# Last inverses on another queue, tables ahead of an exchange, softmax sums behind a score tile

## The chip, the cores and the metric

The kernel runs on one core of a Trainium2 chip. Five engines work side by side, each through a list of instructions in a fixed order, and wait for each other through semaphores: TensorE (PE in the profile; its weight loads are PEld), VectorE (DVE), ScalarE (ACT), GpSimd (POOL) and SyncE (SP). SyncE does nothing here but issue DMAs; GpSimd issues DMAs and does a few elementwise operations. The metric is device time in microseconds from start to end of one execution, as the median of several runs.

## The reference

Two layers stand one behind the other, in float32. The input x has 4 batches of 1024 channels by 1024 pixels (32 x 32); `_rmsnorm` takes the root mean square over all 1024 features.

```python
x = hidden_states.reshape(B, C, N).transpose(0, 2, 1)
qkv = (x @ w_qkv.T + b_qkv).reshape(B, N, 3, nh, hd)        # 16 heads of 64
q, k = _apply_rope(q, cos, sin), _apply_rope(k, cos, sin)   # pairs of features turned by tables
q = _rmsnorm(q.reshape(B, N, inner), q_norm_w).reshape(B, N, nh, hd)
k = _rmsnorm(k.reshape(B, N, inner), k_norm_w).reshape(B, N, nh, hd)
scores = jnp.einsum('bqhd,bkhd->bhqk', q, k) * scale
attn = jax.nn.softmax(scores, axis=-1)
ctx = jnp.einsum('bhqk,bkhd->bqhd', attn, v).reshape(B, N, inner)
out = _rmsnorm(ctx @ w_proj.T, norm_out_w) + residual
```

The second layer is a bottleneck block on the result: a 1x1 convolution to 256 channels, a 3x3 convolution, a 1x1 convolution back to 1024, each followed by a normalisation over the batch, and a scaled residual. The change does not touch it.

## The kernel before

**Stages.** For each batch the kernel makes q, k and v (three projections), then the attention, then the output projection (y). In the profile the products of these are p_q, p_k, p_v, sc and cx (attention) and p_y. Features lie on partitions, 128 to a block, and eight blocks f make the 1024 features; a block holds two heads and is called a head pair, hp. The projections save products by Strassen-like sums: `project2` runs seven outer products k, each of seven inner ones of four matmuls, with sums of weights (made once and kept in DRAM, `wd` and `wd2`) and sums of right-hand sides that VectorE makes just ahead (L450 to L454 for the inner, L281 to L284 for the outer sums). The seven weight tiles of one outer product come from a ring of eight buffers (`wring`), so the next product's weights are loaded as the tiles of the last one are used up. SyncE issues these loads.

**Attention.** It is in two halves c of 512 query pixels and eight head pairs each, sixteen steps for a batch. In a step TensorE makes eight score tiles (L787), each for 128 keys and both heads; ScalarE takes the exponential (L794); VectorE adds the eight results into a tile of partial sums d_ (L798, L800); then TensorE makes the product with v from the same exponentials (cx, L808). What is missing is the sum over the 128 partitions, also a TensorE product, with a tile of ones: `dn`. Four heads (two steps) share one such product (L841), right behind the second step's cx. In the first half of each batch it is done for eight heads at once instead (L861): `halve` first folds each tile's upper partitions onto its lower ones by DMAs on GpSimd's queue (L852 to L855), into tiles called `fold`.

**Inverses.** ScalarE copies dn to SBUF (L891); the rows travel through DRAM (`dens`) into a small tile, VectorE inverts that (`few`), and it travels back; `spread` then loads each inverse onto the 32-partition groups of a tile (inv, eight DMAs), VectorE multiplies the attention's result with it (L764) and GpSimd adds v's bias (L765). All these DMAs are on SyncE. For the last four heads of a batch the detour is left out: VectorE inverts the whole tile (L893), SyncE stores it and spreads it straight from SBUF (L894, L910). This happens within the output projection of that batch, which needs the result for its later products.

**Rotary tables.** `rope` multiplies q (or k) with the sine table into a second tile and with the cosine table in place (`turn`, L718 to L725), then adds the first to the second with partitions swapped, by an accumulating DMA on GpSimd (L727, the exchange). The tables are first multiplied with the inverse root mean square (L715), which destroys them, so behind the last block of each turn GpSimd loads them again (`load_tables`, L176 and L177). `pace["tables"]` keeps the next rope's first step from being put into VectorE's list too early after that load.

**Weight parts.** During batch 0's attention 21 sets of weight sums for later are made (`prepare_blocks`, `prepare`): SyncE loads four tiles, VectorE makes four sums, and the last argument names the queue that stores them.

**Order.** TensorE's, VectorE's, ScalarE's and GpSimd's lists are in the order in which the program writes them. The program hangs VectorE's work of the projections onto product counts (`after`, `waiting`, `pace`). SyncE's list is ordered when the program is built. TensorE's result banks are three score tiles of two banks each, one bank for cx and one for dn.

Of the kernel before, what the change touches and what calls it, by code (L numbers as in the profile page):

```python
# [11 lines left out]
F32 = mybir.dt.float32  # L12
# [6 lines left out]
P = 128  # L19
B, C, H, W = 4, 1024, 32, 32  # L20
N = H * W
NT = C // P
HD = 64
NHP = C // (2 * HD)
CH = 512
# [36 lines left out]
NH = NT // 2  # L62
NG = NT // 2
QH = P // 4
# [21 lines left out]
def program(ctx, tc, x, wblk, w2, w3, vecs, cos, sin, out, bad):  # L86


    nc = tc.nc
# [26 lines left out]
    def col(name, i=0):  # L116
        return vec[:, COL[name] + i : COL[name] + i + 1]
# [40 lines left out]
    with tc.tile_pool(name=f"st{u}", bufs=2) as st, ExitStack() as s:  # L158
# [11 lines left out]
        cosT = tp.tile([P, N], F32, tag="cos", name="cosT")  # L170
        sinT = tp.tile([P, N], F32, tag="sin", name="sinT")

        def load_tables(queue):
            for i in range(2):

                queue.dma_start(sinT[i::2, :], sin[1 - i :: 2, :])  # L176
            queue.dma_start(cosT, cos)  # L177

        ident = None
# [23 lines left out]
        def bank(kind, name):  # L203
            pool, shape = psum[kind]
            return pool.tile(shape, F32, tag=kind, name=name)
# [503 lines left out]
        def rope(b, dst, total, eps, scale, w, tag, biased=True):  # L709

            def tables():
                for t in (sinT, cosT):
                    nc.vector.tensor_tensor(t, t, total, ALU.mult)  # L715

            def turn(f):
                k, other = dst[:, f, :], big_temp(f"{tag}s_{b}_{f}")  # L718
                for i, (t, table) in enumerate(((other, sinT), (k, cosT))):
                    if w is not None:  # L720
                        nc.vector.scalar_tensor_tensor(t, k, w[i][:, f : f + 1], table, ALU.mult, ALU.mult)
                    elif biased:
                        nc.vector.tensor_tensor(t, k, table, ALU.mult)
                    else:
                        nc.vector.scalar_tensor_tensor(t, k, col("bq", f), table, ALU.add, ALU.mult)  # L725
                for i in range(2):
                    nc.gpsimd.dma_start(dst[i::2, f, :], other[1 - i :: 2, :], accum_op=ALU.add)  # L727
                if f == NT - 1 and (b, tag) != (B - 1, "k"):
                    load_tables(nc.gpsimd)
                    pace["tables"] = pace["at"] + 3.7  # L730

            def then():
                if pace["at"] < pace["tables"]:
                    after(pace["tables"] - pace["at"], then)
                    return
                waiting.append((4 * TT, tables))
                for f in range(NT):
                    waiting.append((4 * TT, lambda f=f: turn(f)))

            inverse_rms(total, eps, scale, f"{tag}_{b}", then)  # L740
# [26 lines left out]
        def attention(b, c, q_all, k_all, v, probs_, late, ready, extra, slow, steps_in_all, load_parts, fold):  # L767


            at = half[c]  # L770
            sums_ = []
            for hp in range(NHP):
                n = f"{b}_{c}_{hp}"
                if late:
                    late.pop(0)()
                rows = shifts(q_all, k_all, n, hp, c) if bad is None else None
                probs = []
                if fold and hp % 2 == 0:
                    d_ = fold[hp // 4][:, hp % 4 // 2 * 2 : hp % 4 // 2 * 2 + 2, :]
                else:  # L780
                    d_ = acc.tile([P, 2, CH], F32, tag="tot", name=f"den_{n}")
                for t in range(N // P):
                    p = probs_[:, t]
                    sc = bank("sc", f"sc_{n}_{t}")
                    for j in range(2):
                        d = slice(j * HD, (j + 1) * HD)
                        nc.tensor.matmul(  # L787
                            sc[:, j], k_all[d, hp, t * P : (t + 1) * P], q_all[d, hp, at],
                            start=True, stop=bad is not None,
                        )  # L790
                    if bad is None:
                        for j in range(2):
                            nc.tensor.matmul(sc[:, j], ones[0:1, :], rows[j], start=False, stop=True)
                    nc.scalar.activation(p, sc, AF.Exp)  # L794
                    if t == 3:
                        load_parts()
                    if t == 1:
                        nc.vector.tensor_tensor(d_, probs[0], p, ALU.add)  # L798
                    elif t > 1:
                        nc.vector.tensor_tensor(d_, d_, p, ALU.add)  # L800
                    probs.append(p)
                if eights and eights[0][0] <= c * NHP + hp:
                    eights.pop(0)[1]()
                o = bank("cx", f"cx_{n}")
                for t in range(N // P):
                    for j in range(2):
                        h0 = (2 * hp + j) * HD
                        nc.tensor.matmul(  # L808
                            o[j * HD : (j + 1) * HD, :], v[:, t, h0 : h0 + HD], probs[t][:, j],
                            start=(t == 0), stop=(t == N // P - 1),  # L810
                        )

                nc.scalar.copy(q_all[:, hp, at], o)  # L813
                sums_.append(d_)
                if hp % 2 == 1:
                    for r in ready:
                        mean_of_v(q_all, *r)
                    ready.clear()
                if fold:
                    halve(hp, d_, fold[hp // 4][:, hp % 4 // 2 * 2 : hp % 4 // 2 * 2 + 2, :])  # L820
                    if hp % 4 == 3:
                        eights.append((hp + 2, lambda n=n, hp=hp: sum_of_eight(b, n, hp, fold[hp // 4], ready)))
                if half_done and half_done[0][0] <= c * NHP + hp:
                    half_done.pop(0)[1]()
                if slow:
                    slow.pop(0)()

                if waiting:
                    next_waiting()
                slots = NCH * NHP - 1  # L830
                if extra and steps_in_all == 0 and hp > 0:
                    extra.pop(0)()
                for _ in range(len(extra) - -(-steps_in_all * max(slots - 1 - c * NHP - hp, 0) // slots) if steps_in_all else 0):
                    extra.pop(0)()
                if hp % 2 == 0 or fold:
                    continue
                dn = bank("dn", f"dn_{n}")
                for i, d_ in enumerate(sums_):
                    for j in range(2):
                        q = slice((2 * i + j) * QH, (2 * i + j + 1) * QH)  # L840
                        nc.tensor.matmul(dn[q, :], ones[:, :QH], d_[:, j], start=True, stop=True)  # L841
                sums_ = []
                late.append(lambda *a, n=n, hp=hp, dn=dn: inverses(b, c, hp, n, dn, ready))

        half_done, eights = [], []
        low, high = slice(0, P // 2), slice(P // 2, P)
# [38 lines left out]
        def inverses(b, c, hp, n, dn, ready):  # L885


            r = temp(f"rec_{n}")
            k = 2 * ((b * NCH + c) * NHP + hp - 1)

            nc.scalar.copy(r, dn)  # L891
            if (c, hp) == (NCH - 1, NHP - 1):
                nc.vector.reciprocal(r, r)  # L893
                nc.sync.dma_start(dens[k : k + 4, :], r[::QH, :])  # L894
                spread(c, hp, n, ready, [r[q * QH : (q + 1) * QH, :] for q in range(4)])
                return
            few, rows = to_few(n, k, 4, r[::QH, :])

            def invert():
                nc.vector.reciprocal(few, few)  # L900
                nc.sync.dma_start(rows, few)
                spread(c, hp, n, ready, [dens[k + q, :].partition_broadcast(QH) for q in range(4)])

            half_done.append((0, invert))

        def spread(c, hp, n, ready, rows):
            w = big_temp(f"inv_{n}")
            for i in range(2):
                for j in range(4):
                    nc.sync.dma_start(w[j * QH : (j + 1) * QH, half[i]], rows[2 * i + j // 2])  # L910
                ready.append((c, hp - 1 + i, w[:, half[i]]))

        def o_norm(b, total, ys):
# [245 lines left out]
        load_x(0, 0, range(NH, NT))  # L1159
        w1 += [block(WQ, g, 1, f"q_0_{g}_1") for g in range(NG)]  # L1160
        load_x(0, 1)
        load_tables(nc.sync)
        queue_sums(ts[0], xs[0])
        room = v_room("rq_0")
        for b in range(B):
# [45 lines left out]
            def load_parts():  # L1211

                while todo and len(made) < 2:
                    made.append(todo.pop(0)(pieces, nc.sync, nc.sync))

            extra = [lambda: made.pop(0)()] * len(todo)
            load_parts()
# [8 lines left out]
            slow = [lambda: None] * 3 + [lambda f=f: add_residual(f) for f in range(NT)] if b > 0 else []  # L1226
            probs_ = xp.tile([P, N // P, 2, CH], F32, tag="x", name=f"p_{b}")

            fold = [[tp.tile([P, NH, CH], F32, tag=t, name=f"den_{b}_{t}") for t in ("T0", "T2")], None]
            for c in range(NCH):  # L1230
                if (b, c) == (B - 1, NCH - 1):
                    extra = filters()
# [433 lines left out]
```

## Time and profile before

| | |
|---|---|
| median of 3 runs | 2677.93 us (2675.83 to 2679.2) |
| the profiled execution's own time | 2679.37 us |
| its span, first to last instruction | 2677.6 us |
| TensorE busy | 2646.0 us, 99% |
| VectorE busy | 2112.0 us, 79% |
| ScalarE busy | 1113.8 us, 42% |
| GpSimd busy | 434.3 us, 16% |

The batches' attention stages lie at 288 to 522, 865 to 1096, 1442 to 1673 and 2018 to 2249 us; the output projection follows each. In a row of the profile "p_y L485 <- DMA w_y<-wdf" says that the instruction of line 485 that writes p_y waited for a DMA that fills w_y from wdf. A matmul in float32 shows as two records. Names ending in f (wdf, wd2f, densf) are DRAM tensors of the program.

### The profile page before, as it was taken

What the parts mean: (1) busy time and instruction counts of PE and PEld (TensorE: products, weight loads), DVE (VectorE), ACT (ScalarE), POOL (GpSimd) and SP (SyncE); (2) the same over time, 40 slices, a digit from 0 to 9 for tenths busy, and PEclk for the clock granted to TensorE, in tenths of its full rate; (3) what the DMA queues carried; (4) which work ended last, traced back from release to release, by engine and by line L of the source; (5) the groups of instructions that cost most, each with busy time, mean ns of one, the idle gap of its engine ahead of it and who ended that gap; (6) DMA issues with size and microseconds to landing.
All of it is one profiled execution on the core that took longest, in us unless ns stands there. A gap on an engine that the chain in (4) does not pass through costs nothing. (4 is left out here: it accounts for less than half of the span.)

```text
span 2677.6 us, 32431 instructions
## 1 busy us (share of the span) xinstructions
PE 2646.0 (99%) x11322; PEld 1652.9 (62%) x11322; DVE 2112.0 (79%) x2536; ACT 1113.8 (42%) x1551; POOL 434.3 (16%) x501
## 2 busy tenths in 40 slices
PE   9999999999999999999999999999999999999997
PEld 4448533488888333688886333888884335846843
DVE  5668989997888766888878767887978679877987
ACT  2222455423442555333343555233525554312266
POOL 2542202100111222100111222100111222010000
PEclk9999999999999999999999999999999999999999
DMA  7887787767667551556775441665774443593165
GB/s 279 289 253 216 223 239 239 239 201 221 201 186 204 96 92 34 166 156 218 194 199 131 92 79 30 213 204 175 192 212 87 80 103 105 163 279 115 64 232 208
DMA packets 261387, 462.37 MB, mean 173 GB/s; under 512 B 34528, under 2 KB 127248, under 8 KB 261216
## 3 DMA queue, kind: packets, MB, share of 16 engines
q1 hardware_dynamic: 222048, 328.75, 39.3%
q0 software_dynamic: 39168, 131.45, 20.7%
q8 instruction: 93, 1.52, 0.2%
q14 instruction: 78, 0.64, 0.1%
HBM read 327.43 MB, written 97.01 MB: 159 GB/s over the span
## 5 line engine op out<-in xcount | busy, mean ns | idle before, releaser
L794 ACT ACTIVATE p<-sc 128x1024 f32<-128x1024 f32 x512 | 476.7, 1047 | 26.5 <-PE sc L787 25.8
L787 PE MATMUL sc<-q,k 64*128 64x512 f32 x2048 | 457.7, 596 | 0.0
L800 DVE TENSOR_TENSOR den<-den,p 128x1024 f32<-128x1024 f32 x288 | 356.1, 1236 | 30.4 <-DVE den L800 0.5
L787 PEld LDWEIGHTS sc<-q,k 64*128 64x128 f32 x2048 | 189.9, 186 | 265.2 <-issue 121.7
L808 PE MATMUL cx<-p,to 128*64 128x512 f32 x1536 | 340.2, 595 | 0.0
L808 PEld LDWEIGHTS cx<-p,to 128*64 128x64 f32 x1536 | 106.0, 137 | 228.8 <-issue 228.8
L480 PE MATMUL p_v<-w_v,x 128*128 128x256 f32 x928 | 211.7, 382 | 2.8 <-DVE x L451 2.8
L485 PE MATMUL p_y<-q,w_y 128*128 128x256 f32 x928 | 209.8, 379 | 0.0
L765 POOL TENSOR_SCALAR q<-q,vec 128x512 f32<-128x512 f32 x64 | 128.2, 2014 | 436.3 <-DVE q L764 436.3
L480 PEld LDWEIGHTS p_v<-w_v,x 128*128 128x128 f32 x928 | 177.3, 191 | 28.6 <-DVE x L451 3.9
L485 PEld LDWEIGHTS p_y<-q,w_y 128*128 128x128 f32 x928 | 176.0, 190 | 27.1 <-issue 3.4
L813 ACT COPY q<-cx 128x512 f32<-128x512 f32 x64 | 37.6, 587 | 360.7 <-PE cx L808 360.7
L798 DVE TENSOR_TENSOR den<-p 128x1024 f32<-128x1024 f32 x48 | 59.7, 1245 | 117.5 <-ACT p L794 117.5
L485 PE MATMUL p_q<-to,w_q 128*128 128x256 f32 x672 | 152.2, 379 | 0.0
L485 PE MATMUL p_k<-to,w_k 128*128 128x256 f32 x672 | 152.2, 379 | 0.0
L485 PEld LDWEIGHTS p_q<-to,w_q 128*128 128x128 f32 x672 | 127.4, 190 | 18.4 <-issue 1.2
L485 PEld LDWEIGHTS p_k<-to,w_k 128*128 128x128 f32 x672 | 127.4, 190 | 18.4 <-issue 1.2
L800 DVE TENSOR_TENSOR den_T<-den_T,p 128x1024 f32<-128x1024 f32 x96 | 117.6, 1226 | 10.4 <-ACT p L794 0.5
L808 PE MATMUL cx<-p,rq 128*64 128x512 f32 x512 | 113.4, 595 | 0.0
L1570 PE MATMUL c<-h,w 128*128 128x512 f32 x256 | 110.3, 592 | 0.5 <-ACT h L1473 0.5
L485 PE MATMUL p_y<-to,w_y 128*128 128x256 f32 x384 | 91.3, 383 | 5.8 <-DMA w_y<-wdf 5.8
L480 PE MATMUL p_v<-w_v,t 128*128 128x256 f32 x384 | 90.2, 379 | 0.9 <-DMA w_v<-wdf 0.8
(488 smaller groups left out, 4205.0 us busy)
## 6 DMA issues: line engine op xcount, KB each, us to landing
w_v<-wd2f SPq DMA_DIRECT2D x112, 256.0 KB, 3.3
w_y<-wd2f SPq DMA_DIRECT2D x112, 256.0 KB, 2.8
w_q<-wd2f SPq DMA_DIRECT2D x84, 256.0 KB, 2.7
w_k<-wd2f SPq DMA_DIRECT2D x84, 256.0 KB, 2.7
wd2f<-w_pre SPq DMA_DIRECT2D x68, 256.0 KB, 2.7
x<-in_x_dram SPq DMA_DIRECT2D x64, 256.0 KB, 5.0
q<-qs POOLq DMA_DIRECT2D x64, 256.0 KB, 5.5
k<-ks POOLq DMA_DIRECT2D x64, 256.0 KB, 4.4
```

Source lines behind the costliest of these rows:

```text
L480: nc.tensor.matmul(o[:, q].rearrange("p (g f) -> p g f", g=2), r[:, i, q * P : (q + 1) * P], wt[:, :, i, :], skip_group_check=True, **at,)
L485: nc.tensor.matmul(o[:, q], wt[:, q, i, :], r[:, i, :], skip_group_check=True, **at)
L765: nc.gpsimd.tensor_scalar(cx, cx, col("bv", hp), None, ALU.add)
L787: nc.tensor.matmul(sc[:, j], k_all[d, hp, t * P : (t + 1) * P], q_all[d, hp, at], start=True, stop=bad is not None,)
L794: nc.scalar.activation(p, sc, AF.Exp)
L798: nc.vector.tensor_tensor(d_, probs[0], p, ALU.add)
L800: nc.vector.tensor_tensor(d_, d_, p, ALU.add)
L808: nc.tensor.matmul(o[j * HD : (j + 1) * HD, :], v[:, t, h0 : h0 + HD], probs[t][:, j], start=(t == 0), stop=(t == N // P - 1),)
L813: nc.scalar.copy(q_all[:, hp, at], o)
L1570: nc.tensor.matmul(os[i], w3t[k][f // NH][:, f % NH, :], h2[b, k][:, half[c]], start=(k == 0), stop=(k == NPT - 1),)
```

## The change

- The last inverses of a batch: the store to `dens` and the eight loads of `spread` are issued by GpSimd instead of SyncE.
- Tables: `load_tables` is split. The sines are loaded directly behind VectorE's last product with the sine table, the cosines behind the one with the cosine table, both ahead of the last block's exchange. The due time of the next rope is 5 instead of 3.7 products later.
- Sums of four heads: those with further steps of the same half behind them are held back until the second score tile of the next step is in TensorE's list. The first add into d_ is written behind that. The last sum of a half stays where it was.
- Batch 0's first half makes sums of four heads like the second half, and no longer folds.
- The weight parts of batch 0's attention are stored by GpSimd instead of SyncE.

```diff
-        def load_tables(queue):
+        def load_sines(queue):
             for i in range(2):
                 queue.dma_start(sinT[i::2, :], sin[1 - i :: 2, :])
+
+        def load_cosines(queue):
             queue.dma_start(cosT, cos)
...
+                    if f == NT - 1 and (b, tag) != (B - 1, "k"):
+                        (load_sines, load_cosines)[i](nc.gpsimd)
                 for i in range(2):
                     nc.gpsimd.dma_start(dst[i::2, f, :], other[1 - i :: 2, :], accum_op=ALU.add)
-                if f == NT - 1 and (b, tag) != (B - 1, "k"):
-                    load_tables(nc.gpsimd)
-                    pace["tables"] = pace["at"] + 3.7
+                if f == NT - 1:
+                    pace["tables"] = pace["at"] + 5
...
                     if t == 1:
+                        if fours:
+                            fours.pop()()
+                        if fold and hp % 2 == 0:
+                            d_ = fold[hp // 4][:, hp % 4 // 2 * 2 : hp % 4 // 2 * 2 + 2, :]
+                        else:
+                            d_ = acc.tile([P, 2, CH], F32, tag="tot", name=f"den_{n}")
                         nc.vector.tensor_tensor(d_, probs[0], p, ALU.add)
...
-                dn = bank("dn", f"dn_{n}")
-                for i, d_ in enumerate(sums_):
-                    for j in range(2):
-                        q = slice((2 * i + j) * QH, (2 * i + j + 1) * QH)
-                        nc.tensor.matmul(dn[q, :], ones[:, :QH], d_[:, j], start=True, stop=True)
+
+                def sum_of_four(n=n, hp=hp, sums_=sums_):
+                    dn = bank("dn", f"dn_{n}")
+                    for i, d_ in enumerate(sums_):
+                        for j in range(2):
+                            q = slice((2 * i + j) * QH, (2 * i + j + 1) * QH)
+                            nc.tensor.matmul(dn[q, :], ones[:, :QH], d_[:, j], start=True, stop=True)
+                    return lambda: inverses(b, c, hp, n, dn, ready)
+
                 sums_ = []
-                late.append(lambda *a, n=n, hp=hp, dn=dn: inverses(b, c, hp, n, dn, ready))
+                if hp < NHP - 1:
+                    fours.append(lambda f=sum_of_four: f()())
+                else:
+                    late.append(sum_of_four())
...
-                nc.sync.dma_start(dens[k : k + 4, :], r[::QH, :])
-                spread(c, hp, n, ready, [r[q * QH : (q + 1) * QH, :] for q in range(4)])
+                nc.gpsimd.dma_start(dens[k : k + 4, :], r[::QH, :])
+                spread(c, hp, n, ready, [r[q * QH : (q + 1) * QH, :] for q in range(4)], nc.gpsimd)
...
-        def spread(c, hp, n, ready, rows):
+        def spread(c, hp, n, ready, rows, queue=nc.sync):
...
-                    nc.sync.dma_start(w[j * QH : (j + 1) * QH, half[i]], rows[2 * i + j // 2])
+                    queue.dma_start(w[j * QH : (j + 1) * QH, half[i]], rows[2 * i + j // 2])
...
-                    made.append(todo.pop(0)(pieces, nc.sync, nc.sync))
+                    made.append(todo.pop(0)(pieces, nc.sync, nc.gpsimd))
...
-            fold = [[tp.tile([P, NH, CH], F32, tag=t, name=f"den_{b}_{t}") for t in ("T0", "T2")], None]
+            fold = [None, None]
+            if b > 0:
+                fold[0] = [tp.tile([P, NH, CH], F32, tag=t, name=f"den_{b}_{t}") for t in ("T0", "T2")]
```

More of the change, by code (lines that the diff above doesn't have):

```diff
@@ L770, in attention @@
             at = half[c]
-            sums_ = []
+            sums_, fours = [], []
             for hp in range(NHP):
@@ L777, in attention @@
                 probs = []
[L778 to L781, printed above, removed]
+                d_ = None
                 for t in range(N // P):
@@ L1161, in program @@
         load_x(0, 1)
-        load_tables(nc.sync)
+        load_sines(nc.sync)
+        load_cosines(nc.sync)
         queue_sums(ts[0], xs[0])
```

## The prediction

> **What bounds the kernel now.** I read the page's busy table first, then TensorE's waits, then the timelines around each wait. The busy row settles who sets the time:
>
> ```profile
> PE 2646.0 (99%) x11322; PEld 1652.9 (62%) x11322; DVE 2112.0 (79%) x2536; ACT 1113.8 (42%) x1551; POOL 434.3 (16%) x501
> ```
>
> TensorE lacks 31.6 us of the 2677.6 us span, so an edit counts only if it shortens TensorE's list or removes one of its waits. The list of TensorE's waits (in total us, times, longest):
>
> ```profile
> PE p_y L485 <- DMA w_y<-wdf: 5.8, 4, 2.3
> PE p_v L480 <- DVE x L451: 2.8, 2, 2.0
> PE dn L841 <- DVE den L800: 0.3, 1, 0.3
> ```
>
> The first is once per batch in the output projection, the second in the value projection of batches 2 and 3. Their true price is in TensorE's timeline (start, us, what, count):
>
> ```profile
> 536.28 5.34 PE L485 MATMUL p_y<-y,w_y 128*128 128x256 f32 x24
> 542.58 1.99 PE L485 MATMUL p_y<-to,w_y 128*128 128x256 f32 x8 [0.95 <-DMA w_y<-wdf]
> ...
> 2270.95 2.84 PE L485 MATMUL p_y<-to,w_y 128*128 128x256 f32 x8 [2.29 <-DMA w_y<-wdf]
> ...
> 1407.36 7.13 PE L480 MATMUL p_v<-w_v,x 128*128 128x256 f32 x24 [2.02 <-DVE x L451]
> ```
>
> A matmul of this form starts every 0.216 us. From 536.28, 24 of them end at 541.46; the next starts at 542.58, so 1.12 us is lost. The same sum gives 1.00, 1.85 and 2.45 for the other batches, and 2.17 and 0.99 for the value projection. Each restart costs a further 0.1 (542.58 to the next group at 544.41 is 1.83 for 8, not 1.73). After the two gaps above 2 us it is worse: 24 matmuls from 1407.36 take 6.97 to the next start instead of 5.18, and 16 from 2270.95 take 5.25 instead of 3.46, some 1.7 us more each; after the gap of 1.69 us nothing of the kind. So the output projections lose 6.42 + 0.4 + 1.7 = 8.5 us, the value projections 3.16 + 0.2 + 1.7 = 5.1 us.
>
> What is late in the output projection is SyncE's queue (batch 3):
>
> ```profile
> 2255.92 0.51 SPq L894 DMA_DIRECT2D densf<-rec  x1
> 2256.47 4.99 SPq L910 DMA_DIRECT2D inv<-rec  x8
> 2261.57 2.22 SPq L472 DMA_DIRECT2D w_y<-wd2f  x4
> ```
>
> The last inverses (9 DMAs, waiting for VectorE's reciprocal to end at 2255.9) hold SyncE until 2261.5; the weights behind them go out in a burst, and the one needed at 2268.5 is issued at 2264.4 into a full queue and is there only at 2270.9.
>
> In the value projection it is the sine table, behind the exchange (batch 2, GpSimd, then VectorE):
>
> ```profile
> 1393.75 1.67 POOL L727 DMA_DIRECT2D q<-qs  x2 [10.58 <-issue]
> 1394.85 1.67 POOL L176 DMA_DIRECT2D sinT<-in_sin_dram  x2
> 1395.96 1.09 POOL L177 DMA_DIRECT2D cosT<-in_cos_dram  x1
> ```
>
> ```profile
> 1402.79 1.23 DVE L715 TENSOR_TENSOR sinT<-sinT,sqk 128x1024 f32<-128x1024 f32 x1 [6.51 <-DMA sinT<-in_sin_dram]
> 1404.75 1.23 DVE L715 TENSOR_TENSOR cosT<-cosT,sqk 128x1024 f32<-128x1024 f32 x1 [0.74 <-DMA cosT<-in_cos_dram]
> ```
>
> VectorE stands for 7.2 us, and the sums L450/L451 that TensorE wants next are queued behind. The third loss hides in the sums over keys; the gap of 0.3 understates it. In batch 0 VectorE ends its adds late:
>
> ```profile
> 460.66 1.06 PE L841 MATMUL dn<-den,ones 128*32 128x512 f32 x8
> ...
> 489.83 2.07 PE L841 MATMUL dn<-den,ones 128*32 128x512 f32 x8
> ```
>
> A sum of four heads takes 1.00 us from its start to the next tile's start; here 2.00, at 430.76 1.73, at 520.00 2.36: 3.1 us lost.
>
> **What the skill says.** "TensorE: Matmul & The Clock Gate", Part 1: idle time of about a window of 3.4 us drops the array to half clock, and that window runs freely. The trace agrees in kind (steps of 0.43 instead of 0.216 us), but gaps of 2.0 and 2.3 us were enough. "TensorEngine Tiling (Array Packing)", Key Properties: changing the tiling mode drains the array. The trace agrees: between a pair of score tiles and a pair of the value product the start-to-start step is 0.1 us above the 0.43 within one mode, and the first step in the new mode up to 0.1 more. "DMA: Bandwidth & Descriptors", Issuing engines are not separate DMA queues: DMAs from GpSimd and SyncE share the same 16 engines, and another issuer saves only issue time. That is the very thing lacking at 2256 to 2261; it also warns that bytes brought forward still compete.
>
> **The change part by part.**
>
> Last inverses by GpSimd. Nine DMAs leave SyncE in each batch: 0.51 + 4.99 = 5.5 us and the wait for the reciprocal. The weights of the second product, and with them the third's, are then issued when their buffers come free (every 1.73 us); the built order shows the x loads of the next batch interleaved one by one. For the weight needed at 541.5 the buffer is free at 537.5, 4.0 us ahead, and w_y's median landing is 2.8 us (page, DMA issues); two x loads go out just before it, 0.5 MB, about 1.4 us at the 380 GB/s that the DMA view of this stretch reaches in its busier slices, and most of it has drained by then. I keep 0.3 us in each batch: gain 8.5 - 1.2 = 7.3 us (bounds 3 and 8.5). On GpSimd the nine cost about 0.55 us each (rows L854 555 ns, L919 534, L703 593 to 628), 5.0 us, and a small one lands about 2.6 us after its start (L703 to L704: 625.47 to 628.24). So the last lands near 2255.9 + 5.0 + 2.1 = 2263.0; VectorE's L764 used it at 2263.6. Behind them on GpSimd stand only its own two L765 that wait for L764 anyway. If they come late there is slack: L282 ends at 2269.7 and its result is first wanted at 2271.9, so 2.2 us.
>
> Tables ahead of the exchange. The sines need only VectorE's sine product, the cosines its cosine product: 1390.6 and 1391.9. With the 0.5 us that GpSimd takes to follow, sines start near 1391.1 instead of 1394.85 and cosines near 1392.5 instead of 1395.96, with the 0.5 MB exchange no longer in front: at least 3.4 us earlier. In batch 3 VectorE's two products end at 1969.1 and 1970.4, so sines go 2.4 us earlier than 1972.04 and cosines 2.1 us earlier than 1973.12. VectorE's stop shrinks by as much; TensorE needs 2.2 and 1.0. Gain 5.1 - 0.2 = 4.9 us (bounds 2 and 5.1). The exchange's last head lands 2 us later; it is read in the attention, over 40 us on. The later due time (5 for 3.7) moves nothing: VectorE's order around the tables is the same in both builds.
>
> Sums behind a score tile. Fifteen sums (three in each second half, three in batch 0's first half) now stand between score tiles. Between cx and sc one costs 1.00 us, since a mode change is there anyway; inside sc it brings two changes where there was none. From the steps between matmuls' starts in the trace: 0.52 into it, 0.45 and 0.54 within, 0.53 for the first step out, 2.04 against 0.86 without, 1.18 in all. So 15 x 0.19 = 2.9 us more on TensorE (bounds 0 and 4). Against it, VectorE gets 1.8 us more time: the losses of 0.73 and 1.00 go. The sums at the end of a half stay where they are, among them that of 520.00.
>
> Four heads a sum in batch 0. Two sums of eight (0.99 us each) become four sums of four: 2.0 us more. Twelve DMAs leave GpSimd. VectorE's work is the same, but its products by the inverse come two at a time instead of four, which takes 1.45 us from the stretch before 520; and it no longer waits for the inverse's rows (1.1 us at 475.9) behind stores on SyncE. I leave 0.6 of the 3.1 us: gain 2.5 us (bounds 0 and 3.1).
>
> Parts stored by GpSimd. 84 stores, 0.55 us each, 46 us on an engine that is busy for 40 of these 235 us. They land later (5.8 us for wd2f from GpSimd, 2.7 from SyncE), and the next loads into those buffers wait for it. I worked one round: a part's buffers are wanted again about 11 us after its sums, and a store (5.8) with a load (w_pre lands in 5.0 to 5.4) need about that less the overlap of their four pieces. Cost 0, hidden by that; without it up to 2 us at a few parts, so at most 5 us by way of VectorE.
>
> Sum: 2.9 + 2.0 - 7.3 - 4.9 - 2.5 = -9.8 us. Span 2677.6 - 9.8 = 2667.8; with the 1.8 us around it the execution takes 2669.6 (2679.37 before). That execution was 1.4 above the median, so I predict 2668.2.
>
> **The rivals.**
>
> Weights and parts bound by the transfers: the x loads moved forward keep w_y late (gain 3, not 7.3), and the slower stores hold VectorE in batch 0, so that the 2.5 is lost. For it: DMA engines are 75 to 85% busy in both stretches. Against: SyncE's burst is gone, and the bytes are the same. -9.8 + 4.3 + 2.5 = -3: 2675.
>
> Inverses late from GpSimd, the slower side. If each of the nine took 1.2 us (L176's mean is 1268 ns, L1221's 1334), the last would land 5.8 us later, L282 with it, and TensorE would stand 3.6 us before the second half of the third product, with 1.7 for the slow clock: 21 us over four batches, 2668 + 21 = 2689. It decides once the inverses are more than 2.2 us late, and makes the kernel slower than before from about 4.5 us. Against it: the two sine loads of 1394.85 and the cosines of 1395.96 start 0.55 us apart, so such means overlap.
>
> The deferral alone dear: 0.3 or more each with ScalarE's copy between two exponentials, 2 to 3 us: 2671, still on the forecast's side.
>
> **How the numbers follow.** About 0.2% (5.4 us) is what a measurement can tell from no change. Forecast, with the deferral's rival, 0.60; transfers 0.25, most of it within 0.2%; late inverses 0.10, and 0.05 for a VectorE backlog in batch 0 that costs more than it gains, both mostly slower. Faster 0.62, same 0.25, slower 0.13. Taking out some 0.05 below and 0.12 above, the range is 2663 to 2681; the likeliest case alone spans 2664 to 2672, from the bounds of its terms.
>
> **What would show it.** Right: the w_y wait gone or under 1.5 us in all and no step of 0.43 us there; SyncE's weights following buffers; L715 waiting under 4 us, and no wait on L451; dn inside sc with sc phases near 8.25 instead of 7.07; at 520 no or a small stop. Wrong: a wait of p_y on DVE L282 or L281 (inverses late), DVE L392 waiting for w_pre several us (stores late), or w_y still near 5 us.

## The result and the profile after

The changed kernel takes 2686.26 us (median of 6 runs, 2683.36 to 2688.43) where the kernel before takes 2674.65 beside it (6 runs, 2673.07 to 2679.20): a ratio of 1.0045 with a 95% interval of 1.0034 to 1.0055, some 12 us slower. The forecast of 2668 was wrong in sign, and the result lies above the forecast's range of 2663 to 2681.

The two profiled executions lie closer together than the medians: the one before took 2679.37 us, 4.7 above its median, the one after 2683.36, 2.9 below its own. The busy row of the changed kernel's page:

```profile
PE 2648.4 (99%) x11338; PEld 1651.1 (62%) x11338; DVE 2110.1 (79%) x2538; ACT 1114.5 (42%) x1553; POOL 489.7 (18%) x609
```

TensorE is still the bound and still lacks little: 32.8 us of a span of 2681.2. GpSimd has 55 us more. The list of TensorE's waits shows what remained and what came:

```profile
PE p_y L487 <- DMA w_y<-wdf: 7.8, 4, 2.7
...
PE dn L850 <- DVE den L807: 2.6, 2, 1.8
```

The value projections' wait for VectorE is gone. The wait for the weight in the output projections, which should have vanished, has grown from 5.8 to 7.8, and the sums over keys wait 2.6 where they waited 0.3. In TensorE's timeline the first two stand like this, batch 0 and batch 3:

```profile
541.16 5.34 PE L487 MATMUL p_y<-y,w_y 128*128 128x256 f32 x24
548.08 1.99 PE L487 MATMUL p_y<-to,w_y 128*128 128x256 f32 x8 [1.57 <-DMA w_y<-wdf]
...
2276.24 1.99 PE L487 MATMUL p_y<-to,w_y 128*128 128x256 f32 x8 [2.72 <-DMA w_y<-wdf]
```

I compare stages by TensorE's lost time: the steps from one matmul's start to the next, less 0.216 us each, added up over a projection. Between the two profiled executions the output projections lose 10.8 instead of 8.7 us (+2.1), the value projections 2.0 instead of 7.8 (-5.8). Batch 0's attention takes 239.7 instead of 234.55 us (+5.2; two further executions of the kernel before, shown below, took 234.75 and 233.09), the other three attentions 232.23, 232.04 and 232.32 instead of 231.45, 231.64 and 231.73 (+1.8). That is +3.3 of the 3.6 by which the spans differ.

**Tables.** They come as forecast. VectorE multiplies them in batch 2 almost without standing still (7.2 us before), and TensorE goes on:

```profile
1405.92 1.23 DVE L717 TENSOR_TENSOR sinT<-sinT,sqk 128x1024 f32<-128x1024 f32 x1 [0.30 <-DMA sinT<-in_sin_dram]
1407.95 1.23 DVE L717 TENSOR_TENSOR cosT<-cosT,sqk 128x1024 f32<-128x1024 f32 x1 [0.80 <-DMA cosT<-in_cos_dram]
```

**Weights of the third product.** SyncE is no longer held by the inverses. In batch 3 its list, ordered when the program is built, runs weights and x loads in turn:

```profile
2263.56 0.47 SPq L1123 DMA_DIRECT2D x<-x1df  x1
2264.92 0.38 SPq L385 DMA_DIRECT2D w_y<-in_wblk_dram  x1
2265.35 0.54 SPq L1123 DMA_DIRECT2D x<-x1df  x1
2266.64 2.10 SPq L385 DMA_DIRECT2D w_y<-wdf  x2
```

The needed weight is issued at 2266.64, 12.3 us after this projection began at 2254.3. Before it was 2264.37 after 2249.4, 15.0 us. So the issue did come 2.7 us earlier. But it lands 9.6 us after its issue, at 2276.2, where it took 6.6 before. The view of the DMA engines for 528 to 549 us (batch 0; busy share in tenths, 40 slices) tells why. In the kernel before:

```profile
DMA  9999555423454555849998657999999999989888
```

And the same stretch in the changed kernel:

```profile
DMA  8999999999897999989899999999999999999999
```

Before, the engines had a trough while SyncE gave out the nine small DMAs: 6 x loads were issued in this stretch and 5.36 MB moved. After, there is none: 13 x loads and 6.72 MB. The two rows do not show quite the same part of the stage, since the changed kernel begins this projection 4.8 us later (527.2 for 522.4). Counted from the projection's start, SyncE issues 10 x loads instead of 4 in the first 13 us and 13 instead of 7 in the first 20 us, and 6.3 instead of 5.3 MB move in these 20 us. The needed weight comes behind the ten. The kernel with the inverses alone on GpSimd (below) begins this projection at 522.8, almost where the kernel before does, and its row of the same 21 us has no trough either until the needed weight is there:

```profile
DMA  9999999999999999999999999999999999973982
```

The inverses, now GpSimd's, suffer too:

```profile
2261.88 3.45 POOL L926 DMA_DIRECT2D inv<-rec  x7 [0.20 <-DMA x<-x1df]
2266.32 0.50 POOL L926 DMA_DIRECT2D inv<-rec  x1 [0.99 <-DMA densf<-rec]
```

They are issued 0.5 us apart, as priced, but land a median of 6.9 us after their issue in batch 0 where SyncE's took 2.0.

**Batch 0.** VectorE, which had waited 1.1 us for an inverse's rows in this stage, waits for them seven times (VectorE's waits, 287 to 527 us; total, times, longest):

```profile
DVE few L916 <- DMA few<-densf: 13.5, 7, 3.9
```

One of these times begins with ScalarE's copy of the sum, in its timeline:

```profile
497.04 0.59 ACT L906 COPY rec<-dn 128x512 f32<-128x512 f32 x1 [1.72 <-PE dn L850]
```

GpSimd's timeline of these microseconds:

```profile
496.66 4.20 POOL L769 TENSOR_SCALAR q<-q,vec 128x512 f32<-128x512 f32 x2 [8.19 <-DVE q L768]
500.81 2.19 POOL L399 DMA_DIRECT2D wd2f<-w_pre  x4
```

And SyncE's:

```profile
489.44 16.82 SPq L385 DMA_DIRECT2D w_pre<-wdf  x9
506.68 0.51 SPq L893 DMA_DIRECT2D densf<-rec  x1
509.77 0.34 SPq L897 DMA_DIRECT2D few<-densf  x1
```

The sum is in SBUF at 497.6, but its store leaves SyncE at 506.7: SyncE spends 16.8 us on nine loads of weight parts, which wait for GpSimd's stores out of the same buffers to land (74.8 us of such waits in this stage, 4.3 before). GpSimd gives out four of these stores only at 500.81, behind its own two additions. VectorE then waits until 511.3, its adds end late, and TensorE stands before the second half of the sum:

```profile
523.38 1.05 PE L850 MATMUL dn<-den,ones 128*32 128x512 f32 x4
526.26 1.05 PE L850 MATMUL dn<-den,ones 128*32 128x512 f32 x4 [1.84 <-DVE den L807]
```

### The profile page after: what moved, and what is told of

Its sections match the earlier page's. It is cut to its first block, busy times and chain, and to the rows that moved or that the text cites. A ratio compares the mean times of both kernels' runs of the same rounds, so it can differ in the third digit from the quotient of the medians.

```text
span 2681.2 us, 32605 instructions
## 1 busy us (share of the span) xinstructions
PE 2648.4 (99%) x11338; PEld 1651.1 (62%) x11338; DVE 2110.1 (79%) x2538; ACT 1114.5 (42%) x1553; POOL 489.7 (18%) x609
## 4 chain that ended last, share of the span: by engine, by line
PE 91%; DMA 3%; DVE 3%; issue 1%; ACT 0%; POOL 0%; SPq 0%; DVEq 0%; POOLq 0%; ACTq 0%
PE sc L788 16%; PE cx L815 16%; PE p_v L482 12%; PE p_y L487 11%; PE p_k L487 9%; PE p_q L487 9%; PE c L1589 4%; PE pa_q L305 2%; PE c2x L1440 2%; PE c L1006 2%; PE c2y L1440 2%; DMA w_y<-wdf 1%; PE c L965 1%; PE pc_q L305 1%; PE pa_k L305 1%; PE c1s L1006 1%
## 5 line engine op out<-in xcount | busy, mean ns | idle before, releaser
L807 DVE TENSOR_TENSOR den<-den,p 128x1024 f32<-128x1024 f32 x312 | 383.7, 1230 | 36.9 <-ACT p L795 5.1
L805 DVE TENSOR_TENSOR den<-p 128x1024 f32<-128x1024 f32 x52 | 66.0, 1269 | 111.7 <-ACT p L795 111.7
L807 DVE TENSOR_TENSOR den_T<-den_T,p 128x1024 f32<-128x1024 f32 x72 | 88.2, 1225 | 7.8 <-DVE den_T L807 0.5
L732 POOL DMA_DIRECT2D k<-ks x64 | 57.2, 1064 | 185.4 <-ACT p L795 78.2
```

## The experiments

Every ratio is against the kernel before on the same chip. Losses are summed as above, each from one profiled execution.

### Each part of the change alone

The tables: `load_tables` split, sines and cosines loaded ahead of the last exchange.

```diff
+                    if f == NT - 1 and (b, tag) != (B - 1, "k"):
+                        (load_sines, load_cosines)[i](nc.gpsimd)
```

> The kernel before with the tables' part alone: sines and cosines loaded ahead of the last exchange. If this part works by itself as it was priced, the waits of the value projection on the sums of x go and the time falls by 4.9 us (ratio 0.9982); the trace of the whole change lost 1.96 us in the value projections against 7.80, so up to 5.8. Rival: what is gained there is lost again because the exchange, and all that GpSimd issues behind it, comes later: 0, with a new wait in the attention.

Measured: 2670.87 us, ratio 0.9988 (0.9979 to 0.9996), -3.8 us. The value projections lose 1.7 us; no wait there names VectorE. The part works by itself, though for less than 4.9, and the interval does not exclude 4.9.

The last inverses:

```diff
-                nc.sync.dma_start(dens[k : k + 4, :], r[::QH, :])
+                nc.gpsimd.dma_start(dens[k : k + 4, :], r[::QH, :])
...
+                spread(..., nc.gpsimd)
```

> The kernel before with the nine DMAs of the last inverses on GpSimd instead of SyncE, alone. As predicted: 7.3 us less (0.9973), w_y waits under 1.5 us in all. Theory A (transfers: SyncE, no longer held for 5.5 us, brings the next batch's x forward, and these bytes and the inverses delay the weight of the third outer product): no gain, w_y waits of 6 us or more, the output projections lose 9 to 13 us instead of 8.7, time 0 to 8 us longer. Theory B (the inverses themselves land too late from GpSimd): the wait of p_y names VectorE's product or sum, not w_y.

Measured: 2678.35, ratio 1.0011 (1.0003 to 1.0019), +3.6 us. TensorE's waits:

```profile
PE p_y L485 <- DMA w_y<-wdf: 9.1, 4, 2.6
```

The output projections lose 13.7 us. What was to bring 7.3 us costs some. The wait names the weight and never the inverses' product, which speaks for theory A and against B.

The sums behind a score tile, with the fold kept:

```diff
+                    if t == 1:
+                        if fours:
+                            fours.pop()()
...
+                if hp < NHP - 1:
+                    fours.append(lambda f=sum_of_four: f()())
```

> The kernel before with the sums of four heads behind a score tile, alone (batch 0's first half keeps its sums of eight, parts stored by SyncE). As priced: twelve sums at 0.19, 2.3 us more, less up to 2.5 us of VectorE's stalls in batch 0: 0 to +2.3 (1.0000 to 1.0009). Theory C (the inverse's rows come too late when the sum comes later; VectorE waits for them and holds up its adds): in batch 0 VectorE waits 5 us or more for few and TensorE loses 2 us or more before dn there, in all +4 to +6 us.

Measured: 2675.19, ratio 1.0004 (0.9995 to 1.0012), +0.5 us. Batch 0's attention takes 233.29 us, which another execution of the kernel before reached as well (233.09), so no gain there is shown; the other three take 0.6 longer each. VectorE waits 0.4 us for few. The price is as forecast, and theory C falls: the deferral alone makes no row late.

The parts' stores:

```diff
-                    made.append(todo.pop(0)(pieces, nc.sync, nc.sync))
+                    made.append(todo.pop(0)(pieces, nc.sync, nc.gpsimd))
```

> The kernel before with the weight parts of batch 0 stored by GpSimd, alone. As priced: 0 (0.9995 to 1.0005), VectorE waits for w_pre under 2 us. Theory C in its other form (the stores by GpSimd land later, so the loads of parts hold SyncE longer, and the rows of the inverses behind them come late): VectorE waits 4 us or more for few, batch 0's attention is 2 to 4 us longer.

Measured: 2681.25, ratio 1.0027 (1.0017 to 1.0037), +6.5 us. Batch 0's attention takes 246.1 us in the profile; 8.2 of the 11.6 more are one stop in the middle of a sum that begins at 431.8. GpSimd's timeline ahead of it:

```profile
412.35 0.89 POOL L855 DMA_DIRECT2D den_T<-den  x1 [2.59 <-DMA den_T<-den]
412.92 4.63 POOL L397 DMA_DIRECT2D wd2f<-w_pre  x8
```

And VectorE's, after a stop of 7.6 us:

```profile
427.09 0.69 DVE L392 TENSOR_TENSOR w_pre<-w_pre,w_pre 128x512 f32<-128x512 f32 x1 [7.62 <-DMA w_pre<-in_wblk_dram]
```

Eight stores, whose sums VectorE made between some 404 and 410, are queued on GpSimd behind additions and a fold that waits for an earlier one. The loads into their buffers come later by as much, and VectorE stands for them. That is theory C's other form, by way of w_pre more than of few.

Four heads a sum in batch 0:

```diff
+            fold = [None, None]
+            if b > 0:
+                fold[0] = [tp.tile(...) for t in ("T0", "T2")]
```

> The kernel before with sums of four heads in batch 0's first half, alone. The other four parts alone measured -3.8, +3.6, +0.5 and +6.5 us, together +6.8, where the whole change has about +12. As priced: two sums more at 1.0, +2.0 us, less what VectorE's stalls lose: 0 to +2. If the parts add up, this one must be near +5, with VectorE waiting for few before it can go on and TensorE standing before dn. If it is +2 or less, the parts meet: sums that need their rows at once are held up by the parts' loads only when GpSimd stores these.

Measured: 2670.95, ratio 0.9987 (0.9978 to 0.9995), -4.2 us; neither expectation had a gain. Batch 0's attention is no shorter (234.54): the stalls of 0.7, 1.0 and 1.4 are gone, two sums are added, and the first sum of four, at 315, takes 2.10 instead of 1.00. The parts alone add up to 2.6 us; the whole change costs 12. So the parts do not simply add.

### Do the stores meet the other parts?

All but the stores:

```diff
-                    made.append(todo.pop(0)(pieces, nc.sync, nc.gpsimd))
+                    made.append(todo.pop(0)(pieces, nc.sync, nc.sync))
```

> The changed kernel with the parts stored by SyncE, as before. Theory of added costs: 6.5 us less than the changed kernel (2686.3), about 2680. Theory of parts that meet: 9 us less or more, 2677 or below, VectorE's waits for few in batch 0 fall from 13.5 us to under 5, and its last stalls before dn (2.81 and 3.87) to 2.4 or less. If the stores have nothing to do with the waits for few (the order of SyncE's loads alone makes the rows late), VectorE still waits 10 us or more for few.

Measured: 2678.48, ratio 1.0015 (1.0008 to 1.0021), 8 us less than the change. VectorE's wait for few falls to 0.3 us, batch 0's attention to 234.64, and no sum stalls. What stays is the output projections' loss, 13.3 us. The 8 us lie between the two theories of the expectation (6.5 for costs that add, 9 for parts that meet): taking the stores back ends nearly all waits for few, but saves little more time than the stores cost alone.

### What makes the weights late

In two kernels the next batch's x (in the last batch x1d) is loaded by ScalarE, whose list keeps the program's order, and five products later; the sums made from it follow by as much. The first has the inverses on GpSimd as well, the second is the kernel before apart from that.

```diff
-                            load_x(b + 1, c, (i,))
+                            load_x(b + 1, c, (i,), nc.scalar)
-                    after(3 + 1.5 * j, load)
+                    after(8 + 1.5 * j, load)
...
-                    after(5 + 1.5 * j, lambda i=i: read_back(1, (i,)))
+                    after(10 + 1.5 * j, lambda i=i: read_back(1, (i,), nc.scalar))
```

> The last inverses on GpSimd alone (+3.6 us, output projections lose 13.7 us), and with it the loads of the next batch's x (in the last batch those of x1d) issued by ScalarE, five products later, so that SyncE has only weights there. Theory A (the x loads that SyncE brings forward compete with the third product's weights): the loss in the output projections falls to 4 us or less, w_y waits under 1.5 us in all, time 4 to 7 us under the kernel before (2668 to 2671). Rival (the weights are late through the small inverse copies themselves, nine DMAs in the same stretch): the loss stays at 9 us or more. Rival B (the inverses are late): once w_y is there, p_y waits for VectorE's sum instead, 4 us or more in all.

> The kernel before with the x loads issued by ScalarE five products later and nothing else; SyncE is still held by the nine DMAs of the last inverses. If the weights are late because the inverses hold SyncE (the reading behind the prediction), the loss in the output projections stays near what it is before, 6 to 9 us, and the time within 2 us of the kernel before. If the bytes of x are what delays them, with or without the inverses, the loss falls to 4 us or less and the time by 4 to 6 us.

Measured: the first 2674.16, ratio 0.9998 (0.9990 to 1.0007), the second 2681.48, ratio 1.0025 (1.0014 to 1.0037). With the inverses on GpSimd the output projections lose 0.15 us in all and wait for nothing; with them on SyncE 3.4 us, w_y's waits 2.2. So the same nine DMAs of GpSimd delay nothing once the x loads are elsewhere: theory A holds for the weights, and its two rivals fall. (The inverses land 3.4 to 4.7 us after issue here; whether 6.9 alone would have been too late is not shown, since the weight was later still.) The time does not show it, because five products are too late for the sums that follow. TensorE's waits of the first:

```profile
PE p_q L485 <- ACT q L539: 3.2, 3, 1.1
```

The q projections lose 4.4 us instead of 0.4 in both, and the last stages 3.5 more: 7.5 us that hide the 6 to 8.5 won. The second kernel's +6.3 us is made up in the same way: against the execution of the kernel before that took 2674.9 us (below), its profile has 7.5 us more in these two places and 1.7 in the value projections, and 2.8 less in the output projections, 6.4 in all. The two kernels differ in the inverses' queue alone, and their medians by 7.3 us, which is just what the prediction gave to that step. That agreement is partly luck: in the two profiles 3.3 us of the difference are in the output projections, the rest mostly in the value projections, which the step was not meant for.

### Putting it together

Tables, sums of four heads in batch 0 and inverses by GpSimd, without deferral and GpSimd's stores; x by ScalarE, two products later, and then at the original products:

```diff
-                            load_x(b + 1, c, (i,))
+                            load_x(b + 1, c, (i,), nc.scalar)
-                    after(3 + 1.5 * j, load)
+                    after(5 + 1.5 * j, load)
```

> The kernel before with three parts of the change (tables, sums of four heads in batch 0, last inverses by GpSimd) without the other two (sums behind a score tile, stores by GpSimd), and the x loads by ScalarE two products later. Theory A and the two single results: output projections lose under 1 us, value projections under 2.5, batch 0 has no stall before dn: 2675.1 - 3.9 (fours) - 2 to 4 (tables) - 3.5 to 8 (weights of the third product, at what a median run loses there) gives 2660 to 2666, faster than both kernels. With five products later the first q product waited 1.1 us in each batch and the last stage 3.6 us more; with two these should be under 1 us. Rival: the gains overlap (a run that loses little in the value projections has nothing for the tables to give), 2667 to 2670.

> The same with the x loads by ScalarE at the products where SyncE's program had them, only no longer brought forward by SyncE's list. If it is SyncE's order (x among the weights, as soon as a buffer is free) that makes the weights late, the loss in the output projections is under 1.5 us here too. If the bytes themselves delay w_y whenever they move in that stretch, it is 4 us or more, and the time 4 us over the run with two products later.

Measured: 2665.85, ratio 0.9968 (0.9956 to 0.9980), and 2667.79, ratio 0.9975 (0.9965 to 0.9985): both faster than before and after. The output projections lose 0.15 us in each, so it is not their exact moment that matters to the weights, but that they no longer run ahead in SyncE's list: in the second, 1 or 2 x loads go out in the first 13 us of an output projection with a next batch, against 10 in the changed kernel. The x loads are then also on another issuing queue than the weights. Whether the weights had waited for x in SyncE's own queue or for its bytes on the shared DMA engines is not separated by these runs. The intervals of the two ratios overlap. In the first, the DMA engines over the 21 us that were shown above (batch 0 begins its output projection at 522.8, within 0.5 us of before):

```profile
DMA  7248436959697678765684963646999896422699
```

There is room between the loads, and the inverses land a median of 3.2 us after their issue in this batch, 3.2 to 3.5 in all four.

Tables and sums of four heads alone (both diffs above):

> The kernel before with tables and sums of four heads alone. If the gains add up: 2675.1 - 3.8 - 3.9 = 2667.4. If both shorten the same stalls of the value projections (which lost 1.9 us with the fours alone, against 7.8 in the profile before): 2670 to 2671.

Measured: 2670.66, ratio 0.9986 (0.9979 to 0.9992), -4.2 us: no more than either by itself. VectorE's stops before the tables tell why. In nine profiles of kernels with the old order of the tables, a value projection of batches 1 to 3 loses 0.2 us when VectorE stands there for up to 5.0 us, and from there one us for each further us: 0.9 us at a stop of 5.6, 1.8 at 6.6, 2.1 at 6.9. At 7.2 to 7.4 it is 4.2 to 4.35, with the slow clock. So in these profiles TensorE has 5 us of slack, and of batch 2's stop of 6.9 to 7.4 us only some 2 count. With the sums of four heads alone that stop is 5.6 us, with the inverses alone 5.3, with the stores alone 4.8, though none of these edits touches the tables (why it is shorter there is not shown). Each of these parts takes most of what is to be had here, and in the whole change it can be had only once. Against the execution at 2674.9 us the five parts alone save 8.7 us in the value projections when added up, the whole change 2.6. That is about 6 of the 9 us by which the whole exceeds the sum of its parts; the rest is not traced.

The whole change with x by ScalarE, two products later (the diff of the best kernel laid on the changed one), and the same with SyncE's stores:

> The whole change, with the x loads by ScalarE two products later. Theory A: the changed kernel loses 10.8 us in the output projections, here under 1 us, so 2686.3 - 8 to 10 = 2676 to 2678, about the kernel before; what is left over the kernel without deferral and GpSimd's stores is their cost, 12 us or so. Rival (the delay of w_y is that of GpSimd's DMAs): 2684 or more.

> The whole change with the x loads by ScalarE two products later (2674.8), but the parts stored by SyncE again: all but the stores by GpSimd. If the stores are what costs in batch 0 (VectorE waits 14.0 us for few, attention 240.7 us there), the attention of batch 0 takes 234.6 us as in the other run with deferral and SyncE's stores, VectorE waits under 2 us for few, and the time is 2667 to 2669: 6 to 8 us of the 9 between 2674.8 and 2665.9 are the stores, and 1.8 to 3 the deferral. Rival (the deferral makes the rows late, whoever stores): the attention of batch 0 takes 238 us or more and the time 2672 or more.

Measured: 2674.80, ratio 0.9999 (0.9991 to 1.0007), and 2667.92, ratio 0.9977 (0.9968 to 0.9986). The first loses 0.15 us in the output projections, but batch 0's attention still takes 240.7 us, with VectorE waiting 14.0 us for few. In the second these are 234.6 and 1.1. ScalarE's timeline of the second, at the sum shown above:

```profile
495.11 0.58 ACT L906 COPY rec<-dn 128x512 f32<-128x512 f32 x1
```

And SyncE's:

```profile
496.33 2.00 SPq L385 DMA_DIRECT2D w_pre<-wdf  x4
498.38 0.50 SPq L893 DMA_DIRECT2D densf<-rec  x1
```

The rows leave 2.7 us after the copy, not 9.1. So the account from the changed kernel (2686.3) to the best one (2665.9) is: x loads out of SyncE's list -11.5, stores back on SyncE -6.9, deferral taken out -2.1.

### Are the losses that the forecast counted those of every execution?

The kernel before twice more and the changed kernel once more, nothing edited:

> The kernel before once more, for a second profile of it. In the profile that the prediction was worked out from, the output projections lost 8.7 us and the value projections 7.8, and that execution took 2679.4 where the median of all runs since is 2675. If these losses differ from one execution to the next, this one loses 3 to 6 us less of the two together, as far as its time is below 2679; if they are fixed by the lists, they are the same within 1 us.

> The kernel before a third time, with the same expectation: a loss of 8.7 and 7.8 us if it is fixed, 3 to 6 us less of the two together if it differs between executions and this one takes about 2675.

> The changed kernel once more, for a second profile: the first was its fastest run (2683.4, with 10.8 us lost in the output projections). A median run (2686.3) should lose 13 to 14 us there, as the kernel with the last inverses on GpSimd alone did (13.7), with the value projections near 2 and batch 0's attention near 240 us in both.

Measured: 2674.90, 2676.89 and 2682.07 us. TensorE's waits in the second execution of the kernel before:

```profile
PE p_y L485 <- DMA w_y<-wdf: 5.0, 4, 1.9
PE p_v L480 <- DVE x L451: 1.6, 1, 1.6
```

And in the third:

```profile
PE p_y L485 <- DMA w_y<-wdf: 4.7, 4, 2.4
PE p_v L480 <- DVE x L451: 2.1, 1, 2.1
```

Output and value projections lose 6.2 and 4.6 us in the one, 7.6 and 7.5 in the other, against 8.7 and 7.8 in the profile of the forecast: 10.8, 15.0 and 16.5 together, in the order of their times. They differ between executions. The changed kernel loses 8.3 us in its second profile, where I had expected 13 to 14; that execution too lies below the median, so how much a median one loses there is not shown.

## Why the prediction was wrong, by its own steps

**Last inverses by GpSimd, -7.3 us: this step failed.** The two halves before its flaw were right: SyncE came free, and the weight was issued earlier. Wrong was the sentence that two x loads "go out just before it, 0.5 MB" and that "most of it has drained by then". I counted the two neighbours and not the whole list: with SyncE free, 10 x loads instead of 4 went out in the first 13 us of an output projection (5 instead of 2 in the last batch, where the weight then took 9.6 us to land instead of 6.6) and kept the DMA engines at nine tenths. The inverses on SyncE had been a brake that let the transfers drain. Alone the step measured +3.6 us. Its bounds, 3 to 8.5 us of gain, had no place for a loss, although the rival "weights and parts bound by the transfers" named the mechanism. That rival kept a gain of 3 us; the runs show that its mechanism was right and its size too small.

**The rival "inverses late from GpSimd" did not happen.** They were later than priced (6.9 us after issue, where I had taken 2.6), and VectorE waited 3.7 us for them in batch 0, but TensorE never waited for what follows. With x out of the way, where they landed 3.4 to 4.7 us after issue, it lost 0.15 us.

**Tables, -4.9 us: right in mechanism, a little too large.** 3.8 alone. TensorE's loss fell to 1.7 us. The term was sized on the execution that lost most, and it is no gain of the tables alone: 5 us of VectorE's stop cost nothing, and other edits that shorten the stop below that remove the same loss.

**Sums behind a score tile, +2.9 us: right.** 0.19 us each was forecast; the second halves of batches 1 to 3 grew by 0.4 to 0.8 us for three. Taking the deferral out gave 2.1 us back.

**Four heads a sum, +2.0, and batch 0's stalls, -2.5: close for this stage alone.** Batch 0's attention stayed at 234.5 where I expected 0.5 less, for the first sum's new stop of 1.1; the kernel before itself varies between 233.1 and 234.8 there. The median of the sums of four heads alone fell by 4.2 us all the same. Their profile loses 6.4 us in output and value projections, which the edit does not touch. In the value projections that is VectorE's shorter stop. The output projections lose 4.5 us with this part, 4.5 with the deferral and 3.2 with the stores alone, against 6.2 to 8.7 in the kernel before; why is open. In the whole change the stalls were back, through the next step.

**Parts stored by GpSimd, 0: the second failed step.** It measured +6.5 alone and +6.9 at the end; I had bounded it at 5. I took the store's landing time (5.8 us) and compared it with the round of a buffer, but not the time before its issue: stores stand behind GpSimd's own additions and folds. And I did not ask what is queued on SyncE behind a load that waits for such a store. It is the rows of the inverses, and VectorE's adds wait behind these.

**The base.** The sum was made against one execution, as it must be, but I treated its 16.5 us of losses as those of the median run. 1.4 us was all that I took off; the median of later runs lies 4.7 below that execution.

## What to carry to other kernels

When a queue is relieved, list everything that it will now issue ahead of the transfer you want early, not just the neighbours: a stall in an issuing queue can be what keeps the DMA engines free. If work is moved to another engine's queue, price the wait before its issue as well, and follow each buffer round: who loads into it next, and what else is queued behind that load. Ask how much of another engine's stop TensorE feels before counting it: here the first 5 us cost nothing, and several edits competed for the rest. And read a gain from two or three profiles of the kernel before, since waits of 1 to 2 us can be there in one execution and not in the next.

## What the runs showed of the hardware

Small copies depend on what else is in flight: the 64 KB loads of the inverses landed 2.0 us after issue from SyncE in a trough of the DMA engines, a median of 3.2 from GpSimd with room between the loads, and one of 6.9 with the engines full (batch 0). These runs do not separate the load from the issuer: in the two kernels with x five products later, which differ in the inverses' queue alone, the medians of the four batches are 2.0 to 2.5 us from SyncE, which issues no weights meanwhile, and 3.4 to 4.7 from GpSimd, beside which SyncE's weights go on.

The slow clock after a gap is not a matter of the gap alone. Of 14 stops of TensorE between 2.0 and 2.95 us in the projections of all eighteen profiles, eleven were followed by five to eight steps of 0.43 instead of 0.216 us and three (2.40, 2.67 and 2.72 us) were not; of thirteen stops of 1.5 to 1.93 us none was. The Trainium skill, "TensorE: Matmul & The Clock Gate", Part 1, speaks of idle time of about a window of 3.4 us. These runs show less than a whole window to be enough; that the same gap comes with and without it agrees with the page's free-running window.
